# A conditioned block on one Trainium2 core: TensorE works on zeros from the start, and the gate third of the first conditioning weights is loaded and used later

## The chip, the cores and the metric

The kernel runs on one NeuronCore of one Trainium2 chip. Times are microseconds of device time. The time of a kernel is the median of its runs; the profile is that of one further execution. TensorE is PE in the profile (PEld its weight loads), VectorE is DVE, ScalarE is ACT, GpSimd is POOL, and SyncE is SP. SP issues most of the loads and stores and computes nothing. POOL issues the indirect loads. Every weight and every activation is float32 unless said otherwise.

## The reference

x is 32 x 128 x 512, so 4096 tokens of 512 features. The condition t is 32 x 512, one row for each sequence. The mask is set only for the padded tail of a sequence, at most 32 of its 128 tokens, so few tokens are masked.

```python
m = mask[:, :, None]
emb = silu(t) @ ada_w + ada_b                       # 512 -> 3 x 512
shift, scale, gate_msa = split(emb, 3, axis=1)
norm = layernorm(x) * (1 + scale[:, None]) + shift[:, None]
norm = where(m, norm, 0)
fwd = gelu(norm @ ssm_w1 + ssm_b1) @ ssm_w2 + ssm_b2
bwd = gelu(norm @ bwd_w1 + bwd_b1) @ bwd_w2 + bwd_b2   # the flips cancel
x = x + gate_msa[:, None] * where(m, fwd + bwd, 0)
shift_mlp, scale_mlp, gate_mlp = split(silu(t) @ ffada_w + ffada_b, 3, axis=1)
ff_norm = layernorm(x) * (1 + scale_mlp[:, None]) + shift_mlp[:, None]
return x + gate_mlp[:, None] * (gelu_tanh(ff_norm @ ff_w1 + ff_b1) @ ff_w2 + ff_b2)
```

The first half changes x only where the mask is set. The second half, the feed-forward with 1024 hidden features, is for all tokens.

## The kernel before

**The first half works on slots.** Masked tokens are numbered through all sequences, and the first 512 of them get a slot each. From the mask, small matmuls make the first and the behind-last slot of every sequence (`pb`, `edges`), the rank of a token in its sequence (`pg`, `rank`), the 32 x 512 selection of a sequence by a slot (`pick`), and the token number of each slot (`tokens_of` L212: matmul `pl`, three DVE instructions, `token_i`). POOL gathers the slots' rows of x with indirect loads (L232) into `xc`, 128 slots at a time, in two pairs. The slots are treated in two halves of 256 (`NH`).

**The first conditioning.** `ada_a` holds `ada_w` as four row blocks of 128, each 3 x 512 wide. Its first two thirds (shift and scale) are loaded with four DMAs (L128), its last third (gate) with one DMA of 1 MiB (L130), all on SP before anything else but t. The products with silu(t), `sT`, are `modulation_matmuls` (L251): for each of the four row blocks and each third, one matmul with 32 stationary columns and 512 moving ones, into a 32-partition strip of a PSUM bank. `pm_ss` takes shift and scale, `pm_g` the gate. `modulation_rows` (L262) adds the bias `modb_a` on DVE and writes the rows of `mod1`. `slot_part` (L279) picks these rows out for 128 slots with one more matmul: part 0 is the shift, part 1 the scale, part 2 the gate. The tile `part2` is kept by an ACT copy (`keep_gate`).

**The first layers.** `modulated` (L162) makes xn from xc with two DVE instructions of 128 x 512. `transposed_slots` (L171) transposes it on PE, and ACT copies it to `xT_s`. `hidden` (L178) does the first layers of both directions at once: w1 is 1024 wide, eight blocks `ph` of four matmuls with 256 columns, each followed by an ACT Gelu. Four blocks are of `ssm_w1` and four of `bwd_w1`. `project` (L192) does the second layers, DVE adds bias, gate and xc, and SP stores the result to `x1_rows` in DRAM (`finish_slots` L287). This is done for slots 0 to 255 first (`s0`, `s1`) and, later, for slots 256 to 511 (`s2`, `s3`).

**The feed-forward** follows, in four pairs of four-sequence groups. Before each, x is loaded (L319), and POOL puts the treated rows over it with indirect loads from `x1_rows` (L656; the first eight wait for the stores of `s0` and `s1`). DVE takes the statistics and normalises (L700), xn is turned to feature rows partly by PE (L716), partly by DVE (L1132) and 32-row DMAs (L727), and ACT and DVE scale it (L710, L708). The products are then cut into blocks and done with seven multiplications in place of eight; the block sums of the weights (L308, L577) go to `t_rows` in DRAM and back. More than 512 masked tokens would be treated in a loop at the end.

**What sets the order.** The whole of this is under a manual schedule of all five engines: every engine works in the order of the code. Around the change PE's order is: `pb`, `pg`, transposes of silu(t), `pl`, `pm_ss`, four `part`s, two blocks of `pm_g`, transposes of xn for slots 0 to 127, one block of `pm_g`, `pl` for slots 256 to 511, transposes for slots 128 to 255, the last block of `pm_g`, `ptr_b` (bias columns and slot numbers), three blocks `ph`, parts 1, 0 and 2, the next block. SP's order is: t, `ada_a`, w1 (two DMAs of 1 MiB), w2 (two more), `fw1`, `ada_f` (four DMAs), the biases `b2`, `b2b`, `modb_f` (three DMAs) and `fb2`, `fw2`, four loads of x, then stores. The loads of w1 and w2 wait for one-element memsets by POOL (L464, L468), which stand behind the first pair of gathers in POOL's order.

**Buffers and semaphores.** `ada_f` has the same buffer as `ada_a`, and `modb_f` that of `modb_a`, so their loads wait for the last reader of the former tile: the last `pm_g` matmul and the addition after it. A DMA of SP takes one of eight completion semaphores in turn, and waits for the transfer that had it eight DMAs earlier.

## Time and profile before

| what | value |
|---|---|
| median of 3 runs | 470.43 us (468.7 to 472.58) |
| profiled execution, its own time | 470.92 us |
| its span, first to last instruction | 469.2 us |
| PE busy | 452.4 us, 96% |
| DVE busy | 334.0 us, 71% |
| ACT busy | 174.9 us, 37% |
| POOL busy | 159.4 us, 34% |
| moved by DMA in the span | 70.41 MB, 150 GB/s |
| first `pm_ss` matmul starts | 6.51 us |
| first gather of tokens issued | 8.04 us |
| first-layer matmuls start | 21.18 us |
| `ada_f` loads issued from | 21.05 us |
| stores to `x1_rows` of slots 0 to 255 issued from | 50.51 us |
| first gather from `x1_rows` | 60.80 us |

Busy times of PE include waiting inside its pipeline. A row of the timeline gives start, duration, engine, line, operation, written tile and read tiles, and in brackets how long the engine idled before it and what released it. An indirect or an ordinary DMA is listed under the engine that issues it (SPq, POOLq), with the time of the issue, not of the transfer. A matmul in float32 leaves two records.

### The profile page before, as it was taken

Reading aid. Unit: us, or ns where it says so; the run is one execution under the profiler, and the core shown is the slowest. Engines: PE = TensorE matmul, PEld = TensorE weight load, DVE = VectorE, ACT = ScalarE, POOL = GpSimd, SP = SyncE. Lnnn points to the kernel's source line nnn. Section 1 sums busy time; section 2 is a strip of 40 time slices with the busy share of each in tenths; the row PEclk is TensorE's granted clock in tenths of the full one; section 3 lists DMA queues with packets and bytes.
Section 4 is the critical chain, followed back from the end, with each engine's and each line's share of the span. In section 5 each row is a group of like instructions: output and inputs, shape, how many; then the busy total and the mean of one; then the engine's idle time right before and its main releaser. Section 6 shows DMA issues by size and latency. Waiting matters only on the chain.

```text
span 469.2 us, 5826 instructions
## 1 busy us (share of the span) xinstructions
PE 452.4 (96%) x2000; PEld 365.3 (78%) x2000; DVE 334.0 (71%) x538; ACT 174.9 (37%) x380; POOL 159.4 (34%) x151
## 2 busy tenths in 40 slices
PE   6899999897999999999999999999999999999995
PEld 2475384475878888888888888888888888888884
DVE  4649377999778966997687498967873995434645
ACT  3131022543365074153643712545537134462000
POOL 6200063046876000189740003897100024660000
PEclk9999999999999999999999999999999999999999
DMA  8999943490413861854068528240863341213012
GB/s 278 386 408 362 394 172 53 86 345 19 121 44 134 137 90 49 312 174 163 1 194 106 106 98 288 102 161 3 217 100 88 125 168 62 96 64 117 0 76 107
DMA packets 82194, 70.41 MB, mean 150 GB/s; under 512 B 63136, under 2 KB 63664, under 8 KB 81138
## 3 DMA queue, kind: packets, MB, share of 16 engines
q1 hardware_dynamic: 67298, 57.95, 40.1%
q0 software_dynamic: 4256, 10.75, 6.8%
q10 hardware_dynamic: 10608, 1.32, 2.0%
q8 instruction: 17, 0.28, 0.2%
q14 instruction: 15, 0.12, 0.1%
HBM read 56.83 MB, written 13.17 MB: 149 GB/s over the span
## 4 chain that ended last, share of the span: by engine, by line
PE 61%; POOL 6%; ACT 6%; DVE 5%; issue 2%; POOLq 0%; DVEq 0%
PE a_o L1068 18%; PE e_o L1068 16%; PE a_m L888 14%; PE e_m L888 12%; ACT hb L850 2%; POOL hb L972 2%; ACT ha L850 1%; POOL ha L972 1%; POOL ha L939 1%; POOL rstd L694 1%; DVE xT L827 1%; PE last L1068 1%; DVE sx L817 1%; ACT a_o L1014 1%; ACT e_o L1014 1%
## 5 line engine op out<-in xcount | busy, mean ns | idle before, releaser
L939 POOL TENSOR_TENSOR ha<-p_m,ha 128x512 f32<-128x512 f32 x20 | 27.2, 1361 | 152.7 <-ACT ha L946 143.4
L1068 PE MATMUL e_o<-fw,ha 128*128 128x256 f32 x256 | 57.9, 379 | 0.0
L710 ACT ACTIVATE xT<-xT,modT 128x128 f32<-128x128 f32 x104 | 41.0, 480 | 40.2 <-DMA xT<-xn 39.7
L1068 PE MATMUL a_o<-t,hb 128*128 128x256 f32 x240 | 54.1, 379 | 0.0
L1068 PEld LDWEIGHTS e_o<-fw,ha 128*128 128x128 f32 x256 | 48.6, 190 | 6.6
L1068 PEld LDWEIGHTS a_o<-t,hb 128*128 128x128 f32 x240 | 45.6, 190 | 6.2
L656 POOL DMA_INDIRECT x<-x_rows,slot_i x32 | 36.6, 1144 | 30.2 <-DMA x_rows<-t_s 21.3
L850 ACT ACTIVATE hb<-hb,biasT 128x256 f32<-128x256 f32 x64 | 29.0, 500 | 29.9 <-POOL hb L972 19.3
L939 POOL TENSOR_TENSOR hb<-p_m,hb 128x512 f32<-128x512 f32 x20 | 29.8, 1489 | 18.2 <-DVE hb L918 17.9
L902 ACT COPY p_m<-e_m 128x512 f32<-128x512 f32 x27 | 15.8, 585 | 50.4 <-PE e_m L888 47.1
L946 ACT COPY ha<-e_m 128x512 f32<-128x512 f32 x32 | 18.5, 577 | 30.6 <-PE e_m L888 28.6
L1068 PE MATMUL e_o<-fw,s 128*128 128x256 f32 x128 | 29.2, 381 | 0.5 <-DVE s L1022 0.4
L1068 PE MATMUL a_o<-fw,ha 128*128 128x256 f32 x128 | 29.0, 380 | 0.0
L1068 PE MATMUL a_o<-t,s 128*128 128x256 f32 x128 | 28.9, 379 | 0.0
L184 PE MATMUL ph_s<-xT_s,w 128*128 128x256 f32 x128 | 28.7, 382 | 0.0
L198 PE MATMUL po_s<-w,h_s 128*128 128x512 f32 x64 | 28.5, 592 | 0.0
L1068 PEld LDWEIGHTS e_o<-fw,s 128*128 128x128 f32 x128 | 24.1, 190 | 4.9 <-DVE s L1022 1.7
L184 PEld LDWEIGHTS ph_s<-xT_s,w 128*128 128x128 f32 x128 | 24.0, 190 | 4.7 <-ACT h_s L188 1.5
L1068 PEld LDWEIGHTS a_o<-fw,ha 128*128 128x128 f32 x128 | 24.2, 190 | 3.5 <-ACT a_o L1014 0.2
L1068 PEld LDWEIGHTS a_o<-t,s 128*128 128x128 f32 x128 | 24.3, 190 | 3.3
L913 DVE TENSOR_TENSOR e_m<-a_m,ha 128x512 f32<-128x512 f32 x20 | 13.9, 696 | 17.1 <-POOL ha L939 6.6
L850 ACT ACTIVATE ha<-e_m,biasT 128x256 f32<-128x256 f32 x48 | 20.0, 467 | 14.9 <-PE e_m L888 9.6
(206 smaller groups left out, 878.1 us busy)
## 6 DMA issues: line engine op xcount, KB each, us to landing
tw<-t_rows SPq DMA_DIRECT2D x16, 896.0 KB, 5.2
x<-in_x_dram SPq DMA_DIRECT2D x16, 512.0 KB, 9.3
gate<-gate_rows POOLq DMA_DIRECT2D x8, 1024.0 KB
out_dram<-x SPq DMA_DIRECT2D x15, 512.0 KB, 3.1
xT<-xn SPq DMA_DIRECT2D x92, 64.0 KB, 2.7
fw<-in_L_cond_ff_w_dram SPq DMA_DIRECT2D x2, 2048.0 KB
ada_f<-in_L_cond_ffada_w_dram SPq DMA_DIRECT2D x4, 768.0 KB, 13.6
ada_a<-in_L_cond_ada_w_dram SPq DMA_DIRECT2D x4, 512.0 KB, 5.5
```

What stands on the lines that cost most here:

```text
L184: nc.tensor.matmul(ph[:, :n], w[:, k, ts(f, P)], xT[:, k, :], start=(k == 0), stop=(k == KC - 1))
L198: nc.tensor.matmul(po, h[f][:, ts(i, P)], w[:, f, :], start=(f == 0), stop=(f == HC - 1))
L656: nc.gpsimd.indirect_dma_start(out=xs[i // G][i % G // 2][:, i % 2], out_offset=None, in_=x1_rows[:slots, :], in_offset=bass.IndirectOffse ...
L710: nc.scalar.activation(out, src, AF.Identity, bias=shift, scale=scale)
L850: nc.scalar.activation(dst[:, n], src[:, n], AF.Gelu_apprx_tanh, bias=biasT[:, f : f + 1])
L888: nc.tensor.matmul(bank[:, ts(n, QT)], self.w_block(j, product)[:, ts(n, P)], self.x_block(j, product), start=(product in ("P1", "P5") and ...
L902: nc.scalar.copy(p5, e)
L913: nc.vector.tensor_tensor(e, a, p5, add)
L939: nc.gpsimd.tensor_tensor(self.place(RESULT[j], c), self.p5[j], other, ALU.add)
L946: nc.scalar.copy(self.place(RESULT[j], c), src)
L972: nc.gpsimd.tensor_tensor(part, self.place("21", c), part, ALU.add)
L1068: nc.tensor.matmul(part, src[:, k, ts(i, P)], w[product][:, k, :], start=(last and k == 0), stop=True, skip_group_check=True,)
```

## The change

- A tile `zeros` is filled by DVE's first instruction, and TensorE multiplies it by itself in bfloat16 into a tile that nobody reads: 512, 512, 512, 512 and 256 columns ahead of its first useful work, 256 columns ahead of `pg`, and twice 256 columns ahead of `pl`.
- The gate third of `ada_a` is no longer loaded directly behind the first two thirds. SP issues it between w1 and w2, behind a one-element memset by POOL.
- The eight-record gate product `pm_g` and its addition, before spread over the transposes, now stand together behind the third block `ph` of the first layer.
- On SP, `b2` and `b2b` are issued before `ada_f` and no longer behind it.

The number of useful matmuls, of bytes loaded and of DMAs is the same.

```diff
     def load_ada(w, which, split):
...
-        if split < 3 * D:
-            nc.sync.dma_start(
-                t[:, :, split:], w[:, split:].rearrange("(k p) d -> p k d", p=P)
-            )
         return t
...
+    zeros = tp.tile([P, 2 * D], BF16, tag="t", name="zeros")
+    nc.vector.memset(zeros[:, :512], 0.0)
+
+    def idle_matmuls(*sizes):
+        for n in sizes:
+            nc.tensor.matmul(nothing[:, :n], zeros[:, :P], zeros[:, :n], start=True, stop=True)
+
+    nothing = ps_h.tile([P, 512], F32, tag="h", name="nothing")
+    idle_matmuls(512, 512, 512, 512, 256)
     ident = const.tile([P, P], F32, name="ident")
...
     pg = ps_t.tile([P, 512], F32, tag="tr", name="pg")
+    idle_matmuls(256)
     nc.tensor.matmul(pg[:B, :S], maskT, lower, start=True, stop=True)
...
         nc.tensor.transpose(ptr[:, ts(k, B)], s_sb[:, ts(k, P)], ident[:B, :B])
+    idle_matmuls(256, 256)
...
         nc.gpsimd.memset(part[0:1, 0, 0:1], 0.0)
         nc.sync.dma_start(part, w.rearrange("(k p) f -> p k f", p=P))
+
+    part = ada_a[:, :, 2 * D :]
+    nc.gpsimd.memset(part[0:1, 0, 0:1], 0.0)
+    nc.sync.dma_start(part, ada_w[:, 2 * D :].rearrange("(k p) d -> p k d", p=P))
     for j, w in enumerate((ssm_w2, bwd_w2)):
...
-    pm = ps_o.tile([P, 512], F32, tag="o", name="pm_g")
...
-    modulation_matmuls(pm, ada_a, 2, 3, range(2))
...
-    ada_f = load_ada(ffada_w, "f", 3 * D)
     b2 = ssm.tile([P, D], F32, name="b2")
     b2b = tp.tile([P, D], F32, tag="t", name="b2b")
+    for t, vec in ((b2, ssm_b2), (b2b, bwd_b2)):
+        broadcast_rows(t, vec, nc.sync)
+    ada_f = load_ada(ffada_w, "f", 3 * D)
...
-    for t, vec in ((b2, ssm_b2), (b2b, bwd_b2), (modb_f, ffada_b), (fb2, ff_b2)):
+    for t, vec in ((modb_f, ffada_b), (fb2, ff_b2)):
...
-    modulation_matmuls(pm, ada_a, 2, 3, range(2, 3))
...
-    modulation_matmuls(pm, ada_a, 2, 3, range(3, KC))
...
-    modulation_rows(pm, mod1, modb_a, 2, 3)
...
         h1 += hidden(xT_s, NH, w1, 0, AF.Gelu, "s0", ssm, range(4 * c, 4 * c + 3))
+        if c == 0:
+            pm = ps_o.tile([P, 512], F32, tag="o", name="pm_g")
+            modulation(pm, mod1, ada_a, modb_a, 2, 3)
```

## The prediction, made before the changed kernel was run

> **What bounds the kernel now.** I read the page's chain of work first: it names TensorE (PE) for 61% of the span, nearly all in the feed-forward products after 115 us, which the diff does not touch. Asked for in order of time, the chain begins only at 92.55 us, with the ACT scaling L710 and then DVE's L757. The edits lie before 31 us, so what matters is the path from the start to 92.55 us. I followed it backwards in the waits of the first 90 us:

> ```profile
> POOL x L656 <- DMA x_rows<-t_s: 21.3, 1, 21.3
> ACT xT L710 <- DMA xT<-xn: 12.4, 1, 12.4
> DVE st_s L151 <- DMA xc<-in_x_dram,token_i_s: 7.0, 2, 6.2
> ```

> L710 waits for the blockwise store of xn (landed 86.9 us). That store waits for DVE's transposes (72.1 to 77.1), these for the statistics of x, and these for the gathers of L656, the first of which waits until 60.80 us for the x1_rows stores (columns: total us, times, longest). Who is late with those stores? The second, of t_s1, is issued at 54.7, when DVE has finished t_s1, but lands 5.4 us later, while the quickest x1_rows store lands in 2.0 us. The windows say why (third-last column PE clock, then DMA share and GB/s):

> ```profile
> 14.00:22.00 8.00, 7.45 (x30) 2.92 (x27) 5.71 (x14) 1.34 (x3) 1.78 (x2) 1.00 1.05 385
> 53.00:58.50 5.50, 5.50 (x32) 1.84 (x26) 2.31 (x5) 1.17 (x2) 0.00 (x0) 1.00 1.01 407
> 58.50:62.50 4.00, 4.00 (x19) 3.54 (x20) 3.79 (x13) 0.80 (x2) 1.40 (x2) 1.00 0.04 16
> 82.00:90.00 8.00, 7.04 (x27) 3.57 (x27) 7.86 (x22) 3.06 (x8) 0.00 (x0) 1.00 0.58 105
> ```

> The DMA engines are full from about 3 us to 58.5 us and then stop. The store of t_s1 is the last thing in that stream. So the head of the kernel has two clocks: the DMA stream (everything before 58.5) and PE's order. PE is packed from 21 to 82 us, and in 82 to 90 it idles 8.00 - 7.04 = 0.96 us, 0.45 of it just before the first transposes L716 (82.38), which wait for xn.

> The stretch that the change edits, from the timeline:

> ```profile
> 5.39 1.19 PE L216 MATMUL pl_s<-rank,pick 32*128 32x128 f32 x4 [0.38 <-DVE rank L445]
> 12.08 0.68 DVE L264 TENSOR_TENSOR mod<-pm_ss,modb_a 64x512 f32<-64x512 f32 x1 [2.01 <-PE pm_ss L254]
> 13.64 0.69 DVE L151 BATCH_NORM_STATS2 st_s<-xc 128x6 f32<-128x512 f32 x1 [0.88 <-DMA xc<-in_x_dram,token_i_s]
> 17.78 1.04 PE L254 MATMUL pm_g<-ada_a,sT 128*32 128x512 f32 x2
> 18.75 0.71 PE L216 MATMUL pl_s<-rank,pick 32*128 32x128 f32 x4
> 19.98 1.04 PE L254 MATMUL pm_g<-ada_a,sT 128*32 128x512 f32 x2
> 21.18 5.45 PE L184 MATMUL ph_s<-xT_s,w 128*128 128x256 f32 x24
> ```

> DVE has 0.88 us of idle waiting for the first gathered tokens; two of the four gate matmuls run in PE's idle time at 14.74 to 16.6, the other two stand ahead of pl_s and of the first layer.

> [...] the four pl_s records take 1.19 us at 5.4 and 0.71 us at 18.75, and the weight loads of pm_ss come every 0.85 us until about 10.3 us and every 0.43 after. [...]

> **Part 1: zeros on PE.** The zeros (memset 128x256 as the build has it; the 32x256 memset L364 took 0.27 us) push `upper` and with it POOL's chain by 0.27 us. POOL reaches rank at 2.88 and rank's first user comes after 4.9, so that is hidden. It also starts modb_a's load at 3.1 instead of 2.83; it landed by 9.66 and its sum is needed at 12.08, so hidden. The five opening matmuls have 2304 columns[...]. The 256-column ones [...] fall in gaps of 0.35 and 0.38 us[...]. The gain: [...]1.19 - 0.71 = 0.48 us, so token indices and gathers come 0.48 us earlier [...]. pm_ss gains almost nothing: its last block waits for its ada_a rows until 10.58 (the waits name that DMA), and those are not moved up.

> **Part 2: the gathers.** Now they are issued at 8.04 and 9.39 behind a full queue, and the DMA windows show their bytes at 11.9 to 13.4 us, after the gate part has drained at 12.1. Without it the stream runs empty at about 9.05. A gather at 62.45, beside little traffic, let its reader go after 4.1 us. So 7.56 and 8.9 give 11.7 and 13.0. DVE is busy with mod until 12.76: statistics start at 12.8 instead of 13.64, 0.84 us gained. Bounds: 0 (no gain) and 0.84 (DVE's own order caps it); worse is possible and is a rival.

> **Part 3: the gate matmuls.** Without them between the transposes, the second transpose runs at xn1's end (18.65 - 0.84 = 17.8) instead of 19.39, its ACT copy (0.58) ends at 19.1, and ptr_b follows the token indices (17.8 + 1.07 of DVE work) at 18.9. The first layer starts at about 19.25, not 21.18: -1.93. But four gate matmuls now stand behind its third block, 4 x 0.86 (two records 0.43 apart) = +3.4. The gate row's addition (0.69) follows them, and part2 waits for it with only two selections to cover it (together about 0.5): +0.5 after drain and handover. Queued behind that matmul is the whole first layer; on DVE, behind the addition, only xc2's statistics, whose turn comes with the selections anyway. Sum on PE: -1.9 + 3.4 + 0.5 = +2.0 us from 27.6 us on. Its weights are there: gate part at about 21 us against a use at 24.7.

> **Part 4: SP's order.** ada_f takes ada_a's buffer, so its loads wait for the last gate matmul: 21.05 before, about 28 after. Queued behind it on SP are modb_f, fb2, fw2, the x loads and the stores. But the stream ahead (w1, gate, w2, fw1, b2, b2b) keeps the engines busy to about 34 us, so 6 us of cover. Without that cover each late microsecond would be one of the stream.

> **Part 5: the stream.** It now has a hole: empty at 9.05, while w1 waits for POOL's memset behind both gathers. That was at 10.36, is at 9.9, w1 issued at 10.0. First bytes come about 0.6 us after an issue at the start (1.25 to 1.85), perhaps 0.9: take 10.75. Before, at 13.0, w1 began with 0.17 MB of gather left. After, at 10.75, left are the 1.05 MB gate part and 0.26 MB (one gather through): 1.14 MB more, 2.9 us at 0.39 MB/us. 10.75 + 2.9 - 13.0 = +0.7 us late. Ends: +0.2 (more gathered in the hole) and +1.8 (none[...]).

> **The sum.** The store of t_s1 is issued at 54.7 + 2.0 = 56.7, still before the stream's end at 58.5 + 0.7, so it lands 0.7 later, and so do the gathers, xn, the blockwise store and L710. PE reaches L716 at 81.94 + 2.0 = 83.9 against xn at 82.38 + 0.7 = 83.1: 0.8 late, of which 0.5 goes into the idle time behind it. Together +1.0. From 92.55 on everything follows. The profiled execution took 470.92 (span 469.2), so 471.9; the median of the runs shown, 470.43, gives 471.4.

> **Rivals.**
> - *Nothing measurable at all, or a shade faster* (0.25): the hole is filled by the gathers and DVE absorbs the rest between 93 and 116 us, where PE has 3.4 us of idle. For it: the end at +0.2. 469.9 to 470.7.
> - *PE becomes the bound* (0.17): the gathers meet w1 on the engines instead of a drained queue. The second pair, amid w2 and fw1, took 22.21 to 28.95, 6.7 us. 8.9 + 6.7 = 15.6 instead of 13.6: the first layer starts at about 22, PE is 4.8 late, the t_s1 store is issued at 59.5, past the drain. It decides from about 1.2 us of PE delay beyond the stream's. Price +2 to +3.5: slower, 472.5 to 474.
> - *SP starves the stream* (0.05): if the last gate matmul ended after 34 us, SP would hold ada_f and everything behind. It needs 7 us more than I work out. Each us costs one: 475 or more.
> - *The head gets shorter* (0.08): the zeros and an early first layer bring the whole chain forward by the 1.9 us or more. It needs the x1_rows store to wait for PE and not for the stream; the windows speak against it. 466 to 468.5.

> **How the numbers follow.** My likeliest case (0.45) is 470.5 to 472.5 with 471.4 in it. Three runs of the kernel before spread over 3.9 us, so 1% (4.7 us) is about the least that can be told from no change. The range 467.5 to 474.8 takes in the near-zero rival, most of the PE one and the spread. Faster by over 1% needs a gain that I see nowhere: 0.07. Slower by over 1% is the starved stream and the tail of the PE rival: 0.12. Within: 0.81.

> **What would show it.** pl_s near 0.7 us at its first run; a dip in DMA share between 9 and 11 us; statistics L151 at 12.8; first layer at 19.3; three more first-layer blocks, then eight pm_g records in a row and a wait of part2 for mod; t_s1's store landing at 60.8 with the stream ending at 59.2; L716 waiting little. I am wrong if the gathers land after 14 us, if the DMA share dips between 28 and 58 us, or if the L656 gathers start before 60.8.

## The result, and the profile after

The changed kernel takes 473.83 us (median of 18 runs, 470.88 to 475.85) against 470.88 us (18 runs, 468.07 to 472.58) of the kernel before on the same chip. The ratio is 1.0069, its 95% interval 1.005 to 1.0088: about 3 us slower, where 1 us was forecast. The profiled execution took 475.84 us (span 474.0), 2 us over its own median, while that of before lay on its median. So a path through the two traces has to explain 4.8 us, and the medians 3.

The waits of the first 98 us of the kernel after name the same chain as before, and one wait that is new (total us, times, longest):

```profile
POOL x L668 <- DMA x_rows<-t_s: 21.7, 1, 21.7
ACT xT L722 <- DMA xT<-xn: 11.7, 1, 11.7
PE part_s L270 <- DVE mod L260: 0.8, 1, 0.8
```

The gathers (L656 before, now L668) still wait for the x1_rows stores, and L722 (before L710) for the blockwise store. DVE's wait for the first tokens is gone from the list. New is TensorE's wait for the gate row. The stretches that the prediction showed, now of the kernel after (third-last column PE clock, then DMA share and GB/s):

```profile
14.00:22.00 8.00, 5.90 (x25) 3.86 (x22) 4.98 (x12) 1.25 (x3) 3.08 (x4) 0.74 1.01 366
53.00:58.50 5.50, 5.50 (x18) 2.12 (x19) 0.85 (x2) 0.00 (x0) 0.00 (x0) 1.00 1.05 412
58.50:62.50 4.00, 4.00 (x24) 1.28 (x19) 2.13 (x4) 0.02 (x1) 0.00 (x0) 1.00 0.63 253
82.00:90.00 8.00, 7.74 (x21) 3.39 (x20) 6.51 (x16) 0.00 (x0) 1.05 (x1) 1.00 0.83 122
```

The first row is the one to stop at: TensorE was busy for 5.90 of 8 us (7.45 before), and the clock fell to 0.74 where it had been 1.00. The third shows that the DMA stream no longer ends at 58.5 us: 0.63 in place of 0.04. In part that is the store of t_s1 itself, issued at 60.1 us. In the last, TensorE has little idle time left ahead of the first transposes. The timeline of the same kernel, the edited stretch:

```profile
5.37 1.22 PE L212 MATMUL pl_s<-rank,pick 32*128 32x128 f32 x4
12.39 0.68 DVE L260 TENSOR_TENSOR mod<-pm_ss,modb_a 64x512 f32<-64x512 f32 x1 [1.79 <-PE pm_ss L250]
13.00 0.68 DVE L147 BATCH_NORM_STATS2 st_s<-xc 128x6 f32<-128x512 f32 x1
16.53 0.66 PE L171 MATMUL ptr_s<-ident,xn_s 128*128 128x128 f32 x4 [1.42 <-DVE xn_s L164]
19.94 7.73 PE L180 MATMUL ph_s<-xT_s,w 128*128 128x256 f32 x24 [0.37 <-issue]
27.60 3.62 PE L250 MATMUL pm_g<-ada_a,sT 128*32 128x512 f32 x8
31.26 0.69 DVE L260 TENSOR_TENSOR mod<-pm_g,modb_a 32x512 f32<-32x512 f32 x1 [10.86 <-PE pm_g L250]
33.05 1.13 PE L180 MATMUL ph_s<-xT_s,w 128*128 128x256 f32 x4
```

Read it from the bottom. The fourth first-layer block starts at 33.05; before it started at 27.63, so TensorE is 5.42 us late. The first three blocks start 1.24 us earlier than before, but take 7.73 us in place of 5.45 (+2.28), at a clock that the windows give as 0.50 from 18 to 24 us. The gate product then takes 3.55 us up to the first part, and the wait for its addition costs another 0.83. -1.24 + 2.28 + 3.55 + 0.83 = 5.42. Ahead of the three blocks, TensorE sat idle for 1.42 us before the transposes, where the kernel before had two blocks of the gate product. The windows of the idle stretch and of the blocks (first busy time is TensorE's):

```profile
15.00:17.00 2.00, 0.58 (x6) 0.42 (x4) 1.81 (x3) 0.00 (x0) 0.69 (x1) 1.00 0.91 288
18.00:24.00 6.00, 5.49 (x16) 4.28 (x17) 1.35 (x5) 0.87 (x3) 2.36 (x3) 0.50 1.05 396
```

From there the delay can be followed by its marks (us):

| mark | before | after |
|---|---|---|
| t_s1 done on DVE | 54.65 | 60.08 (+5.43) |
| first gather from x1_rows | 60.80 | 64.83 (+4.03) |
| first DVE sum s of the feed-forward | 92.92 | 97.68 (+4.76) |
| end of the span | 469.2 | 474.0 (+4.8) |

The first gather and the first sum as the timelines have them, before and then after:

```profile
60.80 1.34 POOL L656 DMA_INDIRECT x<-x_rows,slot_i  x1 [21.34 <-DMA x_rows<-t_s]
92.92 1.23 DVE L757 TENSOR_TENSOR s<-xT 128x1024 f32<-128x1024 f32 x1 [0.42 <-ACT xT L710]
```

```profile
64.83 1.07 POOL L668 DMA_INDIRECT x<-x_rows,slot_i  x1 [21.67 <-DMA x_rows<-t_s]
97.68 1.23 DVE L769 TENSOR_TENSOR s<-xT 128x1024 f32<-128x1024 f32 x1 [0.39 <-ACT xT L722]
```

The last step of the table says that nothing after the first sum gave any of it back in these two executions.

### The profile page after: what moved, and what is told of

It is laid out like the page before. It is cut to its first block, busy times and chain, and to the rows that moved or that the text cites. A ratio compares the mean times of both kernels' runs of the same rounds, so it can differ in the third digit from the quotient of the medians.

```text
span 474.0 us, 5847 instructions
## 1 busy us (share of the span) xinstructions
PE 459.0 (97%) x2008; PEld 368.7 (78%) x2008; DVE 334.6 (71%) x539; ACT 174.7 (37%) x380; POOL 160.1 (34%) x152
## 3 DMA queue, kind: packets, MB, share of 16 engines
q0 software_dynamic: 4256, 10.75, 6.7%
## 4 chain that ended last, share of the span: by engine, by line
PE 59%; POOL 7%; ACT 5%; DVE 4%; issue 3%; POOLq 0%; DVEq 0%
PE a_o L1080 18%; PE e_o L1080 15%; PE a_m L900 13%; PE e_m L900 11%; ACT hb L862 2%; POOL hb L984 2%; POOL ha L951 1%; POOL ha L984 1%; POOL rstd L706 1%; ACT ha L862 1%; POOL hb L951 1%; PE last L1080 1%; DVE sx L829 1%; ACT a_o L1026 1%; ACT e_o L1026 1%
## 5 line engine op out<-in xcount | busy, mean ns | idle before, releaser
L722 ACT ACTIVATE xT<-xT,modT 128x128 f32<-128x128 f32 x104 | 40.8, 479 | 39.0 <-DMA xT<-xn 39.0
L668 POOL DMA_INDIRECT x<-x_rows,slot_i x32 | 37.2, 1164 | 29.9 <-DMA x_rows<-t_s 21.7
L862 ACT ACTIVATE hb<-hb,biasT 128x256 f32<-128x256 f32 x64 | 29.0, 501 | 30.0 <-POOL hb L984 19.3
L180 PE MATMUL ph_s<-xT_s,w 128*128 128x256 f32 x128 | 31.0, 404 | 0.4 <-issue 0.4
L180 PEld LDWEIGHTS ph_s<-xT_s,w 128*128 128x128 f32 x128 | 25.7, 203 | 5.8 <-issue 1.2
## 6 DMA issues: line engine op xcount, KB each, us to landing
fw<-in_L_cond_ff_w_dram SPq DMA_DIRECT2D x2, 2048.0 KB, 16.5
```

The source lines that it names most:

```text
L180: nc.tensor.matmul(ph[:, :n], w[:, k, ts(f, P)], xT[:, k, :], start=(k == 0), stop=(k == KC - 1))
L668: nc.gpsimd.indirect_dma_start(out=xs[i // G][i % G // 2][:, i % 2], out_offset=None, in_=x1_rows[:slots, :], in_offset=bass.IndirectOffse ...
L722: nc.scalar.activation(out, src, AF.Identity, bias=shift, scale=scale)
L862: nc.scalar.activation(dst[:, n], src[:, n], AF.Gelu_apprx_tanh, bias=biasT[:, f : f + 1])
```

## The experiments

Each ratio is to the kernel before on the same chip, whose medians were 470.78 to 471.40 us. "Three blocks" is the duration of the first three first-layer blocks, and "s" the start of the first DVE sum of the feed-forward, both of one profiled execution (us).

| kernel | ratio to before, interval | three blocks | t_s1 done | first gather | s |
|---|---|---|---|---|---|
| before | 1 | 5.45 | 54.65 | 60.80 | 92.92 |
| after | 1.0069, 1.005 to 1.0088 | 7.73 | 60.08 | 64.83 | 97.68 |
| e1 zeros only | 1.0034, 1.0019 to 1.0049 | 5.45 | 54.93 | 60.47 | 92.96 |
| e2 gate part only | 1.003, 1.0011 to 1.0049 | 6.90 | 59.09 | 63.21 | 95.25 |
| e3 early load | 1.0097, 1.0064 to 1.013 | 6.83 | 60.70 | 63.50 | 96.13 |
| e4 w1 first | 1.0131, 1.0093 to 1.0168 | 7.33 | 62.23 | 65.02 | 97.80 |
| e5 filler | 1.0059, 1.0037 to 1.0082 | 5.42 | 57.65 | 63.36 | 95.92 |
| e6 gate product twice | 1.0133, 1.0107 to 1.016 | 8.18 | 64.42 | 67.21 | 100.13 |
| e7 before, blocks twice | 1.0017, 0.9998 to 1.0037 | 5.4 + 3.5 | 58.49 | 61.28 | 93.93 |
| e8 before, fw2 late | 0.9953, 0.9932 to 0.9974 | 5.45 | 54.80 | 57.77 | 91.23 |
| e9 after, fw2 late | 1.0093, 1.006 to 1.0125 | 8.23 | 60.87 | 63.88 | 97.57 |
| e10 filler and fw2 late | 1.0046, 1.0028 to 1.0064 | 5.42 | 56.93 | 59.98 | 93.72 |
| e11 e8, additions on DVE | 0.9949, 0.9923 to 0.9975 | 5.45 | 54.42 | 57.38 | 91.20 |
| e12 zeros doubled | 1.0094, 1.006 to 1.0128 | 7.28 | 60.93 | 64.06 | 96.59 |

### The two parts of the change, each alone

e1 adds the zeros to the kernel before. e2 takes them out of the changed kernel, so that only the gate part and the order on SP differ from before.

```diff
+    idle_matmuls(512, 512, 512, 512, 256)
...
+    idle_matmuls(256)
...
+    idle_matmuls(256, 256)
```

> The kernel before with the zero matmuls alone, the gate load and the gate product left where they were. Stream theory (the changed kernel is late because the DMA stream has a hole between 9 and 13 us): no hole here, so 470.9 within 1 us. TensorE theory (it is late because the four gate matmuls stand in front of the first layer and because TensorE, without them between the transposes, idles until its clock falls to half from 18 to 24 us): the gate matmuls still fill the gap, so also 470.9 within 1 us. Rival (the zeros themselves cost, by delaying DVE and POOL or by unsettling the clock): 472 or more. pl_s should again take 1.2 us if zeros do not count as work for the clock, 0.7 us if they do.

> The changed kernel without its zero matmuls. If the gate part carries all of the loss (stream theory and TensorE theory alike): 473.8 within 1 us. If the zeros give something back that the gate part costs: slower than the changed kernel, 475 or more. If the zeros cost: 472 or less.

Measured: 471.98 us (1.0034) and 471.97 us (1.003). 1.0034 x 1.003 = 1.0064 is within the interval of the whole change: by the medians each part costs about half, and neither gains. Neither the stream nor TensorE theory expected that; it fits the rival that the zeros themselves cost, but by what, the marks of e1 don't show: its s is 0.04 us late, and its profiled execution 0.8 us longer than that of before, all of it behind s.

The head of e2 is late, t_s1 by 4.4 us and s by 2.3. Yet the span of its profiled execution is 468.4 us, 0.8 less than that of before: here about 3 us came back behind s. From s to the end it took 373.2 us; the other thirteen traces took 375.2 to 377.9. Most of this is a wait of TensorE near 115 us, 2.4 us in the kernel before and 2.3 in the changed one, that e2 did not have (last section). How many of its runs, which spread from 470.09 to 474.37 us, escaped it is not known. So the 0.3% of e2 is not the price of the gate part alone.

### Closing the hole in the stream

The windows of the kernel after show the forecast dip in the DMA share, but deeper and longer (before, all of these are 0.98 or more):

```profile
9.00:10.00 1.00, 1.00 (x6) 0.25 (x4) 0.32 (x2) 0.00 (x0) 0.70 (x2) 1.00 0.40 103
10.00:11.00 1.00, 1.00 (x6) 0.30 (x4) 0.57 (x1) 0.00 (x0) 1.00 (x7) 1.00 0.66 213
11.00:12.00 1.00, 1.00 (x6) 0.12 (x2) 0.00 (x0) 0.00 (x0) 1.00 (x3) 1.00 0.80 188
12.00:13.00 1.00, 0.34 (x2) 0.00 (x0) 0.61 (x2) 0.00 (x0) 0.14 (x1) 1.00 0.75 168
```

e3 loads the gate part where it was before and leaves its product late. e4 leaves the load late, but issues w1 ahead of the first gathers.

```diff
     ada_a = load_ada(ada_w, "a", 2 * D)
+    nc.sync.dma_start(
+        ada_a[:, :, 2 * D :], ada_w[:, 2 * D :].rearrange("(k p) d -> p k d", p=P)
+    )
```

```diff
-    token_i = find_slots(0)
-    gather_slots(token_i)
-
     for j, w in enumerate((ssm_w1, bwd_w1)):
...
+    token_i = find_slots(0)
+    gather_slots(token_i)
```

> The changed kernel with the gate third loaded directly behind the first two thirds, as before; the gate product stays behind the third block of the first layer. Stream theory: the hole is gone, the stream ends at about 58.5 us, 471 to 472. TensorE theory: the product still stands ahead of the first layer's fourth block and the gap before the first layer is still empty, so the store of t_s1 is issued at 58 us or later and the time stays at 473 to 474.

> The changed kernel with the two w1 loads, and the memsets they wait for, ahead of the first gathers: SP issues them at about 5 us, so the stream has no hole at 9 us. The gathers then share the engines with w1. Stream theory: 471 to 472.5. TensorE theory: the tokens come no earlier and perhaps later, nothing on TensorE is relieved: 473.5 to 475.

Measured: 474.62 and 476.56 us, no gain, and with e4 a loss of 2.7 us against the changed kernel. Both are above what either theory expected. In both, DVE waits again for the gathered tokens (statistics at 13.88 and 14.43 us against 13.00), TensorE idles longer ahead of the transposes (2.46 and 4.10 us), and everything on it is later. So the hole is not what the change loses. It lets the gathers through, and that is worth at least the bytes that it leaves out (more, by e4; the intervals of e3 and the changed kernel overlap).

### TensorE's clock and the gate product

e5 fills the idle time ahead of the transposes with six more multiplications of zeros. e6 does the gate product twice.

```diff
     rows = [(slot_part(c, 1, ps_o, "o"), slot_part(c, 0, ps_h, "h")) for c in range(2)]
+    idle_matmuls(512, 512, 512, 512, 512, 512)
```

```diff
         if c == 0:
             pm = ps_o.tile([P, 512], F32, tag="o", name="pm_g")
+            modulation_matmuls(pm, ada_a, 2, 3, range(KC))
             modulation(pm, mod1, ada_a, modb_a, 2, 3)
```

> The changed kernel with six more multiplications of zeros (512 columns each) behind the four parts, so that TensorE does not idle from 15.1 to 16.5 us before the transposes. Clock theory (the idle stretch lets the clock fall to half, and the first three blocks then take 7.73 us in place of 5.45): the clock row stays at 1.00 from 18 to 24 us, the three blocks take about 5.5 us, everything behind them comes 2.2 us earlier, and the time is 1.5 to 2.2 us below the changed kernel's 473.8, about 472. Stream theory of the prediction (the transfers set the end of the head): the store of t_s1 still lands at about 64 us and the time stays at 473.5 to 474.

> The changed kernel with the eight-record gate product done twice in its new place, the first result thrown away: 3.4 to 3.6 us more of TensorE there and later ada_f loads, nothing else. If TensorE's order sets the end of the head in the changed kernel: the time rises by about all of it, to 476.5 to 477.5. If the stream sets it, the first 1.5 us or so are hidden, and the time is 474 to 475.5.

The timeline of e5 shows the filler and the three blocks, and its window from 18 to 24 us the clock at 1.00:

```profile
15.39 1.47 PE L362 MATMUL nothing<-zeros 128*128 128x512 bf16 x6
19.82 5.42 PE L180 MATMUL ph_s<-xT_s,w 128*128 128x256 f32 x24
```

```profile
18.00:24.00 6.00, 5.25 (x28) 4.33 (x26) 1.69 (x6) 1.83 (x5) 2.36 (x3) 1.00 1.04 394
```

The clock part of the theory holds: without the idle stretch the clock does not fall, and the blocks take 5.42 us. TensorE is 2.43 us earlier at t_s1. Of this only 1.47 reaches the gather, since the store now meets the end of the stream (by an estimate from the gather's start it lands 5.0 us after its issue, in place of 4.0). The time is 473.62 us, a ratio of 1.0059 against 1.0069: a gain of this size can't be told from none here, and it is the 473.5 to 474 that was expected if the stream set the end. e10 below, with the stream out of the way, can tell more.

e6 gives 477.63 us, a ratio 0.64% above that of the changed kernel, or 3 us, for 3.4 us more of gate product. In the two traces t_s1 is 4.34 us later, since the blocks also start 0.46 us later and take 0.45 longer. The first gather is 2.38 us later, s 2.45 and the end 2.4: t_s1's store now lands 2.0 us after its issue in place of 4.0. So the stream hid about 2 us more of TensorE's delay, and what lies beyond counts in full. From the timeline of e6:

```profile
67.21 1.07 POOL L669 DMA_INDIRECT x<-x_rows,slot_i  x1 [21.58 <-DMA x_rows<-t_s]
```

e6 shows the edge of SP's cover, too. ada_f is issued at 35.59, and a gap opens in the stream, in the window of e6:

```profile
34.00:38.00 4.00, 4.00 (x13) 1.37 (x12) 2.27 (x5) 0.50 (x1) 0.50 (x1) 1.00 0.51 165
```

### What bounded the kernel before, TensorE or the stream

e7 delays TensorE alone, in the kernel before, by multiplying two first-layer blocks twice (`again` is a new argument of `hidden`). e8 takes the last 2 MiB away from the stream ahead of the x1_rows stores.

```diff
-            for k in range(KC):
+            for k in list(range(KC)) * (2 if f in again else 1):
...
-        h1 += hidden(xT_s, NH, w1, 0, AF.Gelu, "s0", ssm, range(4 * c, 4 * c + 3))
+        h1 += hidden(xT_s, NH, w1, 0, AF.Gelu, "s0", ssm, range(4 * c, 4 * c + 3), (1, 2))
```

```diff
-    nc.sync.dma_start(fw2, ff_w2.rearrange("(k p) f -> p k f", p=P))
     x_of = {0: load_x(0)}
...
     finish_slots(1, h1, gs[1])
+    nc.sync.dma_start(fw2, ff_w2.rearrange("(k p) f -> p k f", p=P))
```

> The kernel before with the second and third first-layer blocks multiplied twice: 3.6 us more of TensorE ahead of the fourth block (about the delay that the new place of the gate product brings), and no other edit. Prediction's theory (the store of t_s1 is last in a stream that ends at 58.5 us, so that more than 3 us of TensorE delay are mostly hidden): +0.5 to +1.5 us over the kernel before, and the first gather from x1_rows at 61 to 62 us. Rival, TensorE's order bounds already before: +3 to +3.6 us, the gather at about 64 us.

> The kernel before with the 2 MiB load of fw2 issued behind the two x1_rows stores in place of ahead of them, so that the stores meet a drained queue. Prediction's theory (the stream bounds the head): the store of t_s1 lands at about 57 in place of 60 us, the gathers from x1_rows start about 3 us earlier, and the time falls by 1 to 3 us, unless fw2 then comes too late for its own readers. Rival (TensorE's order bounds): gathers earlier in the trace but the time within 0.2% of the kernel before.

From the timeline of e7:

```profile
21.58 8.90 PE L184 MATMUL ph_s<-xT_s,w 128*128 128x256 f32 x40
61.28 1.07 POOL L656 DMA_INDIRECT x<-x_rows,slot_i  x1 [21.53 <-DMA x_rows<-t_s]
```

From the timeline of e8:

```profile
57.77 1.07 POOL L656 DMA_INDIRECT x<-x_rows,slot_i  x1 [18.59 <-DMA x_rows<-t_s]
```

In e7 t_s1 is ready 3.84 us later, and the first gather starts 0.48 us later: the store now meets an empty queue and lands 2.0 us after its issue in place of 5.4. The time rises by 0.17%, less than the 0.5 us expected, with an interval that reaches no change. In e8 TensorE is as before, the gather starts 3.03 us earlier, and the kernel takes 468.86 us, 0.47% less. So in the kernel before the stream did bound this point, and TensorE had about 3.4 us (5.4 - 2.0) to spare.

### Both at once

e9 moves fw2 in the changed kernel as e8 does in the one before. e10 adds the filler of e5 to it.

> The changed kernel with the 2 MiB load of fw2 issued behind the two x1_rows stores, so that TensorE alone can make them late. If both TensorE (t_s1 done at 60.1 us) and the late stream (ending about 3 us later than before) hold the changed kernel back: the first gather from x1_rows at about 63 us in place of 64.8, the time 1 to 2 us below the changed kernel's, 472 to 473. If TensorE alone does: gather and time hardly move, 473.5 to 474.

> The changed kernel with both edits: the six extra multiplications of zeros that keep the clock up, and fw2 loaded behind the x1_rows stores. If clock and stream are together what the change lost besides the gate product itself: the first gather at about 60.6 us, as in the kernel before, the head within 0.5 us of it, and the time 470 to 471.5. If only one of the two counts, no more than the better single edit gives: 472 or above.

Measured: 475.5 us (1.0093), outside both expectations, and 472.89 us (1.0046), above its own. In the profile of e9 the gather comes at 63.88, 1 us earlier than in the changed kernel, though pm_ss ends 0.6 us later and the clock falls for longer (8.23 us for the three blocks). Still, s is only 0.1 us earlier: the rows' rstd follows the first gather by 11.6 us, where it was 10.9, which fits gathers that now share the engines with fw2 (DMA share 0.91 from 62.5 to 66 us, 0.04 in the changed kernel). So this way of freeing the stream brings the changed kernel nothing. It does not show that TensorE alone holds it back, since t_s1 was itself 0.8 us later in this trace, and the time, 1.5 us above what was expected in that case, was not forecast (the intervals of e9 and the changed kernel overlap). In its profile TensorE waits 0.9 us between 205 and 222 us and 0.6 between 295 and 312 for loads of weight sums that the profile of the changed kernel does not show.

From e9 to e10 the filler is the only edit. The ratio falls from 1.0093 to 1.0046, about 2.2 us: with the stream out of the way, keeping the clock up is worth about what the three blocks show (2.8 us in these two traces; a further 1.0 us at t_s1 arose ahead of the filler, where pm_ss ended earlier in e10). The three blocks of e9, and then of e10:

```profile
20.23 8.23 PE L180 MATMUL ph_s<-xT_s,w 128*128 128x256 f32 x24 [0.16 <-issue]
```

```profile
19.11 5.42 PE L180 MATMUL ph_s<-xT_s,w 128*128 128x256 f32 x24
```

The first gather is at 59.98, 0.6 us ahead of the forecast; s is 0.8 us later than before, and the time 2.1 us above before, more than the head explains.

### The zeros doubled, and a long sum on VectorE

e12 more than doubles the opening zeros (5120 columns in place of 2304). e11 takes e8 and moves two additions of the first pair from GpSimd to VectorE.

```diff
-    idle_matmuls(512, 512, 512, 512, 256)
+    idle_matmuls(512, 512, 512, 512, 512, 512, 512, 512, 512, 512)
```

```diff
-            nc.gpsimd.tensor_tensor(self.place(RESULT[j], c), self.p5[j], other, ALU.add)
+            engine = nc.vector if (self.p, j) == (0, 3) else nc.gpsimd
+            engine.tensor_tensor(self.place(RESULT[j], c), self.p5[j], other, ALU.add)
```

> The changed kernel with ten opening multiplications of 512 columns of zeros in place of the five with 2304 columns in all, so that TensorE is at work without a break to about 5.5 us. If the change's zeros failed to raise the speed because they were too short: pl_s runs in about 0.7 us at its first run, and pm_ss loads come every 0.43 us; the gathers are later all the same, since pb waits about 2 us behind the zeros: time 474 to 475. If multiplications of zeros do not raise it at this point at all: pl_s still takes 1.2 us, and the time is 474.5 to 476.

> The kernel before with fw2 behind the stores (468.9 us) and, in the first of the four pairs, two additions of 128x512 (ha, hb behind the third P5 product) on VectorE in place of GpSimd. If VectorE's sum of xT takes 2.9 in place of 0.7 us because GpSimd's two additions run beside it: it takes 0.7 us, TensorE's 2.4 us wait near 113 us shrinks to under 1.2, and the time falls by 0.5 to 2 us to 467 to 468.4. If the long sum has another cause: it stays 2.8 us or longer, and the time is 469 to 470.

The timeline of e12:

```profile
1.26 3.93 PE L362 MATMUL nothing<-zeros 128*128 128x512 bf16 x10 [1.26 <-DVE zeros L358]
6.97 0.68 PE L212 MATMUL pl_s<-rank,pick 32*128 32x128 f32 x4 [0.32 <-DVE rank L452]
```

Behind 3.93 us of zeros pl_s takes 0.68 us; behind the 2.10 us of the change it took 1.22, and 1.19 in the kernel before, which has none. The clock column stands at 1.00 in all three. How long the zeros must last is not shown: no run lies between the two lengths. But pl_s comes 1.6 us later for it, and the time is 475.42 us (1.0094), no better than the changed kernel.

e11 missed its target. The additions beside the long sum at 110 us still run on GpSimd there; the edit moved those of another product. The sum took 2.93 us again, and 468.2 us (0.9949) is no different from e8. That it lies in the range expected of shorter sums is chance, and it settles nothing on that point.

## Why the prediction was right or wrong

The time lay in the range, and the direction was right. But 473.83 is not the likeliest case (470.5 to 472.5); it lies in the rival *PE becomes the bound* (472.5 to 474, chance 0.17), and that rival's own story, late gathers and a first layer at 22 us, is not what happened.

- **The bound of the head: right for the kernel before.** e7 and e8 show it from both sides. What stands ahead of the stores in the stream counts: in e8, with fw2 behind them, the first gather came 3.03 us earlier.
- **Part 1, zeros gain 0.48 us: wrong.** pl_s stayed at 1.22 us, the gathers were issued at 8.04 and 9.39 us to the hundredth as before. That the change's zeros would bring pl_s to 0.71 us was an expectation that no trace had shown: 2.10 us of them did not, 3.93 us did (0.68 us in e12). That the zeros cost nothing was wrong as well (e1: 0.34%). How is not shown. The addition behind pm_ss starts at 12.39 us with zeros and at 11.66 without (e2), but over all traces with the change's zeros it starts between 11.64 and 13.01, and over those without between 11.66 and 12.61.
- **Part 2, statistics at 12.8: right** (13.00), though the gathers were not issued earlier. The hole alone brought their bytes sooner, and DVE went straight from its addition to them.
- **Part 3, PE +2.0 us: this is the step that failed.** Measured +5.42. First layer at 19.94 and not 19.25 (+0.69); the gate product 3.55 and not 3.4 (+0.15); the wait for its row 0.83 and not 0.5 (+0.33); and a term that the sum did not have, 2.28 us of half clock in the first three blocks. Together 3.45, which with the 2.0 is the measured sum to a few hundredths. Two of the four gate matmuls had been seen to run in idle time; overlooked was what their leaving would do to the clock: TensorE was busy for 1.64 us from 15 to 17 us before and for 0.58 after, and the clock from 18 to 24 us was 1.00 before and 0.50 after. e5 fills the idle time, and the three blocks are back at 5.42. The 2.28 is one sample: with the same head, e6 and e9 took 8.18 and 8.23 us for the three blocks.
- **Part 4, ada_f at about 28 us, covered to 34: right in kind.** It was issued at 31.25, the share from 27 to 34 us was 1.03, and e6 shows the cover gone at 35.59.
- **Part 5, stream +0.7 us: right in kind, too small.** By 17 us about 1.0 MB less had been moved, 2.6 us of stream; it drained at about 60.5 in place of 58.5 us. But e3, e4 and e9 show that this is not where the time went.
- **The sum.** It let the stream's delay count and not TensorE's, since 56.7 us lay before the end of the stream. With t_s1 at 60.08, TensorE's delay beyond the spare 3.4 us counts, and what remains of the stream adds to it: t_s1's store landed 4.0 us after its issue, where it took 2.0 in an empty queue (e7). 5.43 - 3.4 + 2.0 = 4.03 us at the first gather. The rival's threshold, 1.2 us beyond the stream's delay, was too low: e7 hid 3.4 of 3.84 us.

**What stays open.** The marks of the head explain 4.8 us between two profiled executions, the medians show 3. Over all kernels, s and the median agree only to about 1.5 us: one profile is one sample of runs that spread over up to 6 us. So that TensorE's late head makes the kernel slower is shown (e6, e10 against e9); how much of the 3 us it makes is not. Why zeros alone cost 0.34% with an unmoved head (e1), and e10 more than its head, is not settled; the waits for weight-sum loads that some traces show between 200 and 310 us (0.8 us in e1) may be part of it, and so may a second fall of the clock near 120 us (last section), but no run isolates them.

## What to carry to other kernels

A small product in an engine's idle time can do more than use that time: before moving it, ask what TensorE's clock does in the gap that it leaves. Here 6.8 us of the work that followed ran at half clock. Where two streams of work meet at one point, find the spare time of each by delaying one and relieving the other (e7, e8), before pricing an edit that moves both. The version that beats both kernels came from that test and not from the change: the load that nobody needs yet goes behind the store that everybody waits for (468.86 us, 0.9953).

## What the runs showed of the hardware that was not expected

```profile
14.40:17.80 3.40, 1.98 (x12) 0.94 (x8) 3.03 (x7) 0.57 (x1) 0.72 (x1) 1.00 0.96 327
```

- **The fall lasted 6.8 or 10.2 us.** By the clock column of windows of 0.1 us (after) or 1 us (e9, e12) it lasted 6.8 us in after and e9 and 10.2 us in e12. At the end of the wait of the next point it came again: half clock for 3.4 us in the traces of before (116.1 to 119.6 us) and after (120.2 to 123.7), and for as long, by an estimate from the mean clock of 0.83, between 120 and 130 us in e9 and e12. e1 and e10 had neither fall: their mean granted clock over the whole span was 1.000. The second fall may be one reason why executions of one kernel differ: of the 44 of the kernel before beside e1, the 26 with a mean granted clock of 0.997 or more have a median of 470.54 us, the other 18 one of 471.5.
- **A VectorE sum of 0.7 us that takes 2.8.** From the timeline of the kernel after, and then of e2:

```profile
116.30 1.29 POOL L951 TENSOR_TENSOR ha<-p_m,ha 128x512 f32<-128x512 f32 x1
116.52 2.84 DVE L839 TENSOR_TENSOR xT<-xT,xn_sy 128x512 f32<-128x512 f32 x1
117.53 1.27 POOL L951 TENSOR_TENSOR hb<-p_m,hb 128x512 f32<-128x512 f32 x1
120.36 2.07 PE L900 MATMUL e_m<-xn_sy,tw 128*128 128x256 f32 x4 [2.30 <-DVE e_m L944]
```

```profile
114.10 0.68 DVE L828 TENSOR_TENSOR xT<-xT,xn_sy 128x512 f32<-128x512 f32 x1
115.68 1.29 POOL L940 TENSOR_TENSOR ha<-p_m,ha 128x512 f32<-128x512 f32 x1
116.91 1.28 POOL L940 TENSOR_TENSOR hb<-p_m,hb 128x512 f32<-128x512 f32 x1
```

Where GpSimd's two additions run first, the sum ends 0.56 us after the second of them, and TensorE then waits 2.3 us. So it is in the traces of before, e5, e8, e10, e11 and e12, too: a sum of 2.83 to 2.94 us and a wait of 2.3 or 2.4. In e2, GpSimd came later (its gathers had begun later and taken longer), the sum took 0.68 us, and the wait was gone. That GpSimd's additions hold up VectorE's sum is the author's estimate, from these overlaps and from e2; e11, which was to test it, did not reach these additions, so the cause is not shown.
